# Fourth layer of a graph network: first products evicted 512 edges at a time, with one PSUM buffer more for the second products

## The chip, the core and the metric

The kernel runs on one core of a Trainium2 chip. The metric is the device time of one execution in microseconds (us), lower is better. Five engines work beside each other, each in the order of its own queue, and wait for one another through semaphores: PE (matrix products), DVE (vector work), ACT (activations, copies and casts), POOL (here only the issue of gathers and scatters) and SP (here only the issue of transfers). PE writes its products to PSUM, a small memory of its own, from which DVE and ACT read.

## What is computed

Four graph layers run over the same 12,500 nodes of 32 features and 400,000 edges sorted by their target. Each layer normalizes the nodes, forms a message for each edge, sums the messages of a node and adds the sum to it. The change lies in the fourth layer. Its edges carry 8 scalars, which a small network of two layers (8 to 256 to 256) turns into four 8x8 weight matrices for each edge:

```
h = relu(edge_scalars @ (fc_w1 / sqrt(8))) * sqrt(2)      # (E, 256): the first products
w = (h @ (fc_w2 / sqrt(256))).reshape(E, 4, 8, 8)         # (E, 256): the second products
x = node_features[edge_src]
s1, v1 = x[:, :8], x[:, 8:].reshape(E, 8, 3)
out_s = A * (einsum('eu,euw->ew', s1 * s2, w[:, 0]) + einsum('eui,ei,euw->ew', v1, v2, w[:, 1]) / sqrt(3))
out_v = B * (einsum('eu,euw,ei->ewi', s1, w[:, 2], v2) + einsum('eui,euw->ewi', v1 * s2, w[:, 3]))
node_out = segment_sum(concat(out_s, out_v), edge_dst)
```

Here s2 and v2 are the one and the three parts of the edge's 4 attributes.

## The kernel before

The fourth layer is `edges3` (from line 1252). It works in 196 windows of 2048 edges, that is 16 tiles of 128 edges, and is written out in full, without a loop at run time. For each window:

- `fetch` (SP) loads the window's edge data, `gather` (line 1274, POOL) issues one indirect transfer for each of the 16 tiles that brings the source nodes' features into `hs`. `hs` has four buffers, and the source calls `gather` two windows ahead; POOL itself goes on as soon as a buffer is free.
- `hidden(c, m, h)` forms the first products. The 256 hidden values are two halves m, the 2048 edges four quarters of B = 512. One call takes one m and two quarters: two matmuls of 512 columns (line 1285, `ps_h`) into a PSUM tile of 2 x 512 values on each partition, and one ACT instruction (line 1287) that applies relu to all 1024 and writes them to `hid`. The tile has one buffer (`ph`). Four calls make a window's `hid`.
- `product(c, g)` forms the second products of four tiles (a group g, 0 to 3): eight fp32 matmuls of 256 columns (line 1310, `ps_w`, each of them two records in the profile) into a tile of 4 x 256 values on each partition, of which there are two buffers (`pw`). Then DVE multiplies them with the gathered features in three instructions: `pa` (line 1314), `ps` (1316) and `pv` (1318). `ps` is the last to read `hs` of a group.
- `scalars` (lines 1293 to 1299, DVE) prepares `q`, `dd` and `vv` of the next window. `outputs` (1326 to 1334, DVE) sums `pa`, `pv` and `ps` of a finished window to its messages `f`.
- `thirds` splits `f` into three bf16 parts, in turns of ACT (line 472, a cast) and DVE (lines 474 and 476): cast, subtract, cast, subtract, cast.
- `places` (lines 1340 and 1341, ACT) makes the one-hot matrices `oh` from the edges' targets, with which `collect` (line 1346, PE) sums the messages into the nodes of the window; ACT copies the sums (1349), PE folds the three parts (1352), ACT copies again (1354) and sends the block to memory (`put_late`, lines 489 and 490).

The source goes through the windows with four steps s each. Step s calls `product` and `places` for this window, a part of `outputs`, `thirds`, `collect` and `add` for the last one, and `hidden` for the next one:

```python
for s in range(4):
    if now:
        product(now, s)
        places(now, 4 * s, 4 * s + 4)
    if c:
        ...
    if c + 1 < NW:
        hidden(cs[c + 1], s % 2, s // 2)
        if s == 3:
            scalars(cs[c + 1])
```

That is not the order in which the engines run it. A scheduler in the framework puts the instructions of each engine into a fixed order when the program is built, and it knows the number of buffers in each pool. For a window in the middle of the layer PE's order before is: the 16 matmuls of the collect, a `ps_h` pair, the fold, group 0, a `ps_h` pair, group 1, a `ps_h` pair, group 2, a `ps_h` pair, group 3. DVE's order is: group 3's three products of the window before, the sums (1326, 1327), group 0, the sum 1330, group 1 between 1332 and 1334, line 474, group 2, line 476, `q` and `dd`, group 3. ACT has the first cast of line 472 after the second eviction that follows the collect, and the second cast after the third.

Of the kernel before, what the change touches and what calls it, by code (L numbers as in the profile page):

```python
# [8 lines left out]
F32 = mybir.dt.float32  # L9
BF16 = mybir.dt.bfloat16  # L10
I32 = mybir.dt.int32
AF = mybir.ActivationFunctionType
ALU = mybir.AluOpType
AX = mybir.AxisListType
PSUM = bass.MemoryType.PSUM

P = 128
# [9 lines left out]
B = G * CG * P // Q4  # L27
# [29 lines left out]
class GNN:  # L57
# [1194 lines left out]
    def edges3(self):  # L1252

        nc, tc, CT = self.nc, self.tc, self.CT
        with ExitStack() as ctx:
# [1 line left out]
            gp = ctx.enter_context(tc.tile_pool(name="gather3", bufs=4))  # L1257
            wp = ctx.enter_context(tc.tile_pool(name="work3", bufs=2))
            ph = ctx.enter_context(tc.tile_pool(name="ph3", bufs=1, space=PSUM))
            pw = ctx.enter_context(tc.tile_pool(name="pw3", bufs=2, space=PSUM))  # L1260
            ps = ctx.enter_context(tc.tile_pool(name="ps3", bufs=1, space=PSUM))

            def fetch(c):
# [14 lines left out]
            def hidden(c, m, h):  # L1278

                if (m, h) == (0, 0):  # L1280
                    c["hid"] = wp.tile([P, 2, CT, Q4, 32], F32, name="hid")
                t = ph.tile([P, 2, B], F32, name="ps_h")
                for q in range(2):
                    e0 = (2 * h + q) * B
                    nc.tensor.matmul(t[:, q, :], lhsT=self.w1s[:, m * P : (m + 1) * P],
                                     rhs=c["emb"][:, e0 : e0 + B], start=True, stop=True)
                nc.scalar.activation(c["hid"][:, m, :, 2 * h : 2 * h + 2, :].rearrange("p b q s -> p q b s"),  # L1287
                                     t.rearrange("p q (b s) -> p q b s", s=32), AF.Relu)

            def scalars(c):  # L1290
                hs, sh = c["hs"], c["sh"]
# [71 lines left out]
            for s in range(4):  # L1363
                hidden(cs[0], s % 2, s // 2)
            scalars(cs[0])
            for c in range(NW + 1):
                now = cs[c] if c < NW else None
                if c + 4 < NW:
                    fetch(cs[c + 4])
                if c + 2 < NW:  # L1370
                    gather(cs[c + 2])
# [5 lines that stand above are left out]
                        last = cs[c - 1]  # L1377
                        if s == 0:
                            outputs(last)
                            self.thirds(wp, last, 0)  # L1380
                        elif s == 1:
                            self.thirds(wp, last, 1)
                            self.thirds(wp, last, 2)
                        elif s == 2:
                            self.thirds(wp, last, 3)
                            collect(last)
                        else:
                            add(last)
# [4 lines that stand above are left out]
# [156 lines left out]
```

## Time and profile before

| | |
|---|---|
| median of 3 runs | 20,938.48 us (20,915.86 to 20,953.58) |
| the profiled execution's own time | 20,931.77 us |
| its span, first to last instruction | 20,930.0 us |
| PE, DVE, ACT, POOL busy over the span | 60%, 61%, 31%, 70% |
| fourth layer, its gathers (line 1274) | 3125 gathers, 3017.6 us busy, 966 ns of one |
| second products (line 1310, PE) | 12,544 records, 3194.7 us busy |
| eviction of the first products (line 1287, ACT) | 784 x 1023 ns, 802.0 us busy |
| DVE's three products (lines 1314, 1316, 1318) | 784 x 689, 418 and 951 ns |

The profile is one execution on the chip. Its page has the busy time of each engine, the span in 40 slices with the clock that PE was granted, the DMA queues, the chain that ended last, and groups of like instructions. The trace behind it answers further: the waits (which instruction waited for which, in total, how often, the longest), the timeline of an engine in a stretch of time, and busy times by stretch. A line of the timeline gives start, duration, engine, source line, operation, the tiles by name (written <- read), the shapes, how many records were merged, and in brackets how long the engine sat idle before it and what ended that.

### The profile page before, as it was taken

How to read it: one execution, taken by the hardware profiler on the slowest of the kernel's cores; microseconds unless marked ns; L12 is line 12 of the kernel's file. 1: busy time of each engine (PE TensorE's matmuls, PEld its weight loads, DVE VectorE, ACT ScalarE, POOL GpSimd, SP SyncE). 2: the span in 40 equal slices, each digit the busy share in tenths (PEclk: the TensorE clock that was granted, in tenths of full speed). 3: DMA queues.
4: the chain of work that ended last, by engine and by line, in shares of the span. 5: the costliest groups of instructions: out<-in, count | busy, mean ns of one | idle time of the engine just before them, and what ended most of it. 6: DMA issues, size and time to landing. Idle time of an engine off the chain costs nothing.

```text
span 20930.0 us, 189759 instructions
## 1 busy us (share of the span) xinstructions
PE 12599.4 (60%) x56444; PEld 6767.2 (32%) x56444; DVE 12740.1 (61%) x25505; ACT 6408.9 (31%) x13844; POOL 14745.9 (70%) x12508
## 2 busy tenths in 40 slices
PE   2443433334766666666666666666637777777776
PEld 2333433331211111111111111111125555555554
DVE  3554444334766666666666666666746666666666
ACT  0001110002333333333333333333324444444444
POOL 5777777774788888888888888888755555555553
PEclk9999999998777777777777777777768888888888
DMA  2113332112444444444444444444411111111111
GB/s 96 46 45 111 113 91 74 23 23 72 98 89 90 88 91 90 89 89 90 90 90 90 90 90 90 90 90 90 92 39 23 23 23 23 23 23 23 23 23 30
DMA packets 1482594, 1406.96 MB, mean 67 GB/s; under 512 B 1055751, under 2 KB 1250897, under 8 KB 1426409
## 3 DMA queue, kind: packets, MB, share of 16 engines
q1 hardware_dynamic: 668550, 1143.45, 17.2%
q0 software_dynamic: 750000, 205.60, 12.0%
q10 hardware_dynamic: 62992, 45.63, 0.7%
q8 instruction: 448, 7.34, 0.1%
q14 instruction: 604, 4.94, 0.1%
HBM read 1156.82 MB, written 236.20 MB: 67 GB/s over the span
## 4 chain that ended last, share of the span: by engine, by line
DVE 27%; issue 20%; PE 15%; POOL 14%; another core or an unknown queue 13%; ACT 7%; DMA 4%; DVEq 0%; ACTq 0%; SPq 0%; POOLq 0%
DVE z L853 6%; POOL acc L1008 5%; POOL hs L809 5%; PE ps_w L1310 5%; POOL hs L535 4%; PE ps_y L850 4%; DVE pv L1318 1%; DMA hs<-feat,src_all 1%; PE ps_o L860 1%; ACT oh L1340 1%; DVE f L1327 1%; DVE pa L1314 1%; ACT X L834 1%; PE ps_sum L1346 1%
## 5 line engine op out<-in xcount | busy, mean ns | idle before, releaser
L1008 POOL DMA_INDIRECT acc<-summed,rows x3125 | 5141.5, 1645 | 999.8 <-issue 882.0
L1274 POOL DMA_INDIRECT hs<-feat,src_all x3125 | 3017.6, 966 | 2462.6 <-DVE ps L1316 1460.3
L535 POOL DMA_INDIRECT hs<-feat,src_all x3125 | 3375.3, 1080 | 1368.4 <-issue 864.4
L809 POOL DMA_INDIRECT hs<-feat,src x3125 | 3210.6, 1027 | 1190.2 <-issue 944.4
L1310 PE MATMUL ps_w<-w2b,hid 128*128 128x256 f32 x12544 | 3194.7, 411 | 68.8 <-issue 53.4
L853 DVE TENSOR_TENSOR z<-ps_y,hid 128x1024 f32<-128x1024 f32 x2352 | 2837.7, 1214 | 411.2 <-PE ps_y L850 161.2
L850 PE MATMUL ps_y<-X,w2t 64*128 64x512 f32 x4704 | 2380.0, 744 | 1132.0 <-DVE z L853 656.2
L1310 PEld LDWEIGHTS ps_w<-w2b,hid 128*128 128x128 f32 x12544 | 2577.7, 209 | 625.8 <-issue 85.8
L850 PE MATMUL ps_y<-Q,w2t 64*128 64x512 f32 x4704 | 1677.6, 838 | 1678.1 <-DVE z L853 1163.8
L460 PE MATMUL ps_win<-m,oh 128*128 128x32 f32 x6272 | 1472.7, 400 | 854.9 <-ACT m L664 211.4
L472 ACT CAST f<-f 128x512 bf16<-128x512 f32 x784 | 481.2, 614 | 4785.3 <-DVE f L878 3878.6
L860 PE MATMUL ps_o<-z,sums 128*32 128x512 f32 x9408 | 1746.1, 700 | 30.0 <-DVE r L865 21.4
L460 PEld LDWEIGHTS ps_win<-m,oh 128*128 128x128 f32 x6272 | 1396.3, 328 | 927.7 <-issue 528.3
L690 PE MATMUL ps_deg<-olo,ohi 128*125 128x100 bf16 x3136 | 462.8, 298 | 2001.6 <-DVE olo L687 1416.9
L1287 ACT ACTIVATE hid<-ps_h 128x1024 f32<-128x1024 f32 x784 | 802.0, 1023 | 2368.0 <-remote 1923.5
L1314 DVE TENSOR_TENSOR pa<-ps_w,q 128x512 f32<-128x512 f32 x784 | 540.1, 689 | 1605.5 <-remote 1407.0
L824 DVE STREAM_TRANSPOSE X<-hs 128x512 f32<-128x512 f32 x392 | 273.4, 700 | 1999.8 <-DMA hs<-feat,src 1328.8
L850 PEld LDWEIGHTS ps_y<-Q,w2t 64*128 64x128 f32 x4704 | 521.2, 256 | 2923.8 <-DVE z L853 1578.9
L850 PEld LDWEIGHTS ps_y<-X,w2t 64*128 64x128 f32 x4704 | 614.2, 210 | 2343.2 <-DVE z L853 1159.5
L663 DVE TENSOR_TENSOR m<-hs,edge_attr 128x128 f32<-128x128 f32 x784 | 228.3, 291 | 1609.6 <-issue 779.8
L664 ACT ACTIVATE m<-m 128x128 f32<-128x128 f32 x784 | 240.3, 310 | 3145.1 <-DVE m L663 1175.9
L690 PEld LDWEIGHTS <-ohi 128*125 128x125 bf16 x3136 | 445.7, 215 | 1990.8 <-DVE ohi L687 1035.7
(207 smaller groups left out, 19667.1 us busy)
## 6 DMA issues: line engine op xcount, KB each, us to landing
has<-loc_t SPq DMA_DIRECT2D x392, 1024.0 KB
srow<-in_src_t SPq DMA_DIRECT2D x392, 512.0 KB
N<-n_t SPq DMA_DIRECT2D x3136, 32.0 KB
hs<-feat,src_all POOLq DMA_INDIRECT x6250
emb<-pp SPq DMA_DIRECT2D x252, 280.0 KB
emb<-emb SPq DMA_DIRECT2D x196, 360.0 KB
emb<-pp SPq DMA_DIRECT2D x252, 224.0 KB
emb<-emb SPq DMA_DIRECT2D x196, 288.0 KB
```

The source lines that it names most:

```text
L460: nc.tensor.matmul(c["sum"], lhsT=oh[:, k, :], rhs=feat[:, k, :], start=t0 + k == 0, stop=t0 + k == self.CT - 1)
L535: self.nc.gpsimd.indirect_dma_start(out=t[:, k, :], out_offset=None, in_=self.feats[l][:], in_offset=bass.IndirectOffsetOnAxis(ap=idx[:, t ...
L690: nc.tensor.matmul(c["deg"][:NP, :J], lhsT=ohi[:, k, :], rhs=olo[:, k, :], start=t0 + k == 0, stop=t0 + k == self.CT - 1)
L809: nc.gpsimd.indirect_dma_start(out=c["hs"][:, k, :], out_offset=None, in_=self.feats[1][:], in_offset=bass.IndirectOffsetOnAxis(ap=c["src" ...
L850: nc.tensor.matmul(y[:, q, :], lhsT=self.w2t[64 * q : 64 * q + 64, h, j, :], rhs=c["Q" if j < 3 else "X"][64 * q : 64 * q + 64, h, :], sta ...
L853: nc.vector.tensor_mul(z, y, c["hid"][:, 2 * h : 2 * h + 2, :])
L860: nc.tensor.matmul(c["o", j // 3][32 * q : 32 * q + 32, :], lhsT=self.sums[:, j, :], rhs=c["z", j, q % 2][:, q // 2, :], start=j % 3 == 0, ...
L1008: nc.gpsimd.indirect_dma_start(out=self.tabs[2][k % NTAB][:], out_offset=bass.IndirectOffsetOnAxis(ap=c["rows"][:, G * g + k : G * g + k + ...
L1274: nc.gpsimd.indirect_dma_start(out=c["hs"][:, k, :], out_offset=None, in_=self.feats[3][:], in_offset=bass.IndirectOffsetOnAxis(ap=c["src" ...
L1287: nc.scalar.activation(c["hid"][:, m, :, 2 * h : 2 * h + 2, :].rearrange("p b q s -> p q b s"), t.rearrange("p q (b s) -> p q b s", s=32), ...
L1310: nc.tensor.matmul(w[:, k, :], lhsT=c["hid"][:, m, 4 * g + k].rearrange("p q s -> p (q s)"), rhs=self.w2b[:, m, :], start=m == 0, stop=m == 1)
L1314: nc.vector.tensor_mul(c["pa"][:, gs], w[:, :, 0:128].rearrange("p g (w u) -> p g w u", u=16), c["q"][:, gs, None, :].to_broadcast([P, 4, ...
```

## The change

The PSUM tile of the first products shrinks from two quarters to one, and each matmul of 512 columns has an eviction of its own, so that a window has eight evictions of 128x512 in place of four of 128x1024. The tile still has one buffer. The PSUM that this frees goes to a third buffer for the second products' tile. The sums, the products and the data are the same.

```diff
-            pw = ctx.enter_context(tc.tile_pool(name="pw3", bufs=2, space=PSUM))
+            pw = ctx.enter_context(tc.tile_pool(name="pw3", bufs=3, space=PSUM))
...
-                t = ph.tile([P, 2, B], F32, name="ps_h")
-                for q in range(2):
-                    e0 = (2 * h + q) * B
-                    nc.tensor.matmul(t[:, q, :], lhsT=self.w1s[:, m * P : (m + 1) * P],
-                                     rhs=c["emb"][:, e0 : e0 + B], start=True, stop=True)
-                nc.scalar.activation(c["hid"][:, m, :, 2 * h : 2 * h + 2, :].rearrange("p b q s -> p q b s"),
-                                     t.rearrange("p q (b s) -> p q b s", s=32), AF.Relu)
+                for q in range(2 * h, 2 * h + 2):
+                    t = ph.tile([P, B], F32, name="ps_h")
+                    nc.tensor.matmul(t, lhsT=self.w1s[:, m * P : (m + 1) * P],
+                                     rhs=c["emb"][:, q * B : (q + 1) * B], start=True, stop=True)
+                    nc.scalar.activation(c["hid"][:, m, :, q, :], t.rearrange("p (b s) -> p b s", s=32), AF.Relu)
```

The scheduler's order moves with it. In what follows h0 to h7 are the eight single `ps_h` matmuls of a window in the order in which PE has them after the change. PE then has, with the number of `ps_w` matmuls between them: the collect, the rest of group 0, h0, 2, h1, 5, h2, 3, h3, 5, h4, 2, h5, 6, h6, 1, h7, 2, and the next collect. From h1 on each of them waits for an eviction by ACT. ACT has the evictions of h4 and h5, then both casts of line 472, then the evictions of h6 and h7. DVE has `q` and `dd` after group 3, the sum 1327 (now line 1325) after group 0, and else the order above.

## The prediction

> **What bounds the kernel now.** I read the page first: the fourth layer fills the slices from about 15,400 us on, and there no engine is full. The busy times by stretch say the same: in 15,600 to 20,700 us PE is busy 3654 of 5100 us, DVE 3296, POOL 2860, ACT 2360. So this stage is bound by waits, and I read the waits of that stretch next (waiter, releaser, us in total, times, longest).
>
> ```profile
> ACT hid L1287 <- remote: 1737.7, 287, 11.5
> POOL hs L1274 <- DVE ps L1316: 1347.7, 178, 11.2
> DVE pa L1314 <- remote: 1272.6, 222, 10.2
> ...
> PEld ps_w L1310 <- DVE ps L1316: 78.8, 76, 1.0
> ...
> PEld ps_w L1310 <- DVE pv L1318: 16.9, 33, 1.0
> PE ps_w L1310 <- DVE pv L1318: 10.1, 42, 0.5
> ```
>
> PE's waits for a free ps_w buffer, which a third buffer would remove, are 79 + 17 + 10 = 106 us. The great waits are others: "remote" on DVE and ACT, 3010 us together, and POOL waiting for DVE. "Remote" means that no instruction of the profile ends where the wait ends. In the program both waiters wait for PE alone, so I put one window (512 x 4 edges, one turn of the loop) of PE, DVE, ACT and POOL side by side (start, duration, idle before).
>
> ```profile
> 18262.31 3.72 PE L1310 MATMUL ps_w<-w2b,hid 128*128 128x256 f32 x16 [0.54 <-issue]
> 18265.86 0.60 PE L1285 MATMUL ps_h<-emb,w1s 72*128 72x512 bf16 x2
> 18266.40 3.72 PE L1310 MATMUL ps_w<-w2b,hid 128*128 128x256 f32 x16
> 18278.75 1.94 PE L1346 MATMUL ps_sum<-oh,f 128*96 128x128 bf16 x16 [8.64 <-DVE f L476]
> ```
>
> ```profile
> 18266.26 0.68 DVE L474 TENSOR_TENSOR f<-f,f 128x512 f32<-128x512 f32 x1
> 18276.21 0.69 DVE L1314 TENSOR_TENSOR pa<-ps_w,q 128x512 f32<-128x512 f32 x1 [9.27 <-remote]
> ...
> 18278.02 0.68 DVE L476 TENSOR_TENSOR f<-f,f 128x512 bf16<-128x512 f32 x1
> ...
> 18279.29 0.69 DVE L1314 TENSOR_TENSOR pa<-ps_w,q 128x512 f32<-128x512 f32 x1
> ```
>
> ```profile
> 18265.51 0.62 ACT L472 CAST f<-f 128x512 bf16<-128x512 f32 x1
> 18276.26 1.02 ACT L1287 ACTIVATE hid<-ps_h 128x1024 f32<-128x1024 f32 x1 [10.13 <-remote]
> 18277.18 0.61 ACT L472 CAST f<-f 128x512 bf16<-128x512 f32 x1
> ```
>
> ```profile
> 18253.44 0.94 POOL L1274 DMA_INDIRECT hs<-feat,src_all  x1 [7.25 <-DVE ps L1316]
> ...
> 18272.38 0.95 POOL L1274 DMA_INDIRECT hs<-feat,src_all  x1 [0.30 <-issue]
> 18280.57 0.95 POOL L1274 DMA_INDIRECT hs<-feat,src_all  x1 [7.25 <-DVE ps L1316]
> ```
>
> PE finished group 2's products at 18,266.03 and the next ps_h pair at 18,266.46, yet DVE and ACT are released at 18,276.2, both at once. The word from PE (the event that tells a waiter that a product is done; its arrival is the waiter's start) is some 10 us late. What that moment goes with is POOL's stream of 16 gathers: it starts at 18,253.44, ends at 18,273.33, and 2.9 us later all held words arrive. I went through all 196 windows with the stream's start as zero. Words that PE sends up to about +7 are prompt; those of +8.5 arrive at +10 to +12, those of +10 to +11 at +14 to +20, and of those after +14 nearly all at +22.8. The four groups of a window (0 to 3) reach DVE 0, 3.3, 4.6 and 0 us late on average. The last windows, whose gathers are over, are the proof from the other side:
>
> ```profile
> 20779.35 1.06 PE L1346 MATMUL ps_sum<-oh,f 128*96 128x128 bf16 x16
> ...
> 20797.62 1.06 PE L1346 MATMUL ps_sum<-oh,f 128*96 128x128 bf16 x16
> ```
>
> There a window takes 18.3 us; with gathers it takes 27.2 (18,253.44 to 18,280.57; the median of all periods is 27.19). Why the words are late I can't see in the trace; that they are, and when, I can.
>
> So a period is a ring: DVE's last `ps` of a window frees an `hs` buffer, POOL starts its 16 gathers (20.0 us with their gaps), at +22.8 PE's words come through, and then the **tail** runs until DVE's last `ps`: 80.57 - 76.21 = 4.36 us. 22.8 + 4.4 = 27.2. Only the tail is the kernel's to change, unless PE's words no longer fall into the late stretch.
>
> **The change, part by part.** I take the orders from the built programs of both kernels, engine by engine.
>
> *Third ps_w buffer.* Removes at most the 106 us above; beside the ring it is worth nothing by itself, since PE stands idle 8.6 us waiting for L476 with two full buffers (the PE lines above). What it gives is order: PE's group 0 of the next window stands partly ahead of the collect, and DVE's q and dd (L1291, L1293 of the new file) stand behind group 3's products, not between L476 and them. That takes 79.29 - 78.62 = 0.67 us out of the tail (78.62 is L476's start and 0.60, its pitch).
>
> *ps_h in one bank, evicted by 512.* 784 evictions of 128x1024 (1023 ns) become 1568 of 128x512. That shape is not in the trace for this operation; the nearest row is L472's 128x512 cast, 614 ns, and half of 1023 is the lower bound, 512. I take 614: 4 x 2 x 0.614 = 4.9 us of ACT in a window in place of 4.1. ACT is busy 46% here, so 0.8 us is hidden, except where an eviction stands in the tail. PE's work is the same 8 matmuls.
>
> *The added waits.* With one bank, each of 8 ps_h matmuls waits for ACT's eviction of the one before; in the old kernel 4 pairs did. In the new PE order they stand 2 to 6 ps_w matmuls apart: group 0, h0, 2, h1, 5, h2, 3, h3, 5, h4, 2, h5, 6, h6, 1, h7, 2, collect. A word to ACT that is late now stops PE, with all products behind it. From the rows (0.43 us a ps_w matmul, 0.22 a ps_h one, some 0.2 until its end is known, ACT's one-hots 0.30 and L1341 0.61 from start to start), with the stream's start as zero: the collect waits for h7's eviction and ends at +0.4; fold, four products of group 0 and one of group 1 bring h0 to +3.3, h1 (after h0's eviction) to +4.4, five products h2 to +6.8. Its eviction stands behind L1341 and five one-hots, +7.5 to +8.0; three products later h3 is sent, its word at +8.7. Group 2 ends at +10.7. By the lateness above h3 reaches ACT at +10.7, its eviction ends at +11.3, h4's word goes out at +11.7 and arrives between +17 and +22.8. So h5 goes out at +18 or later and **reaches ACT at +22.8**. That step carries the forecast.
>
> *What stands behind h5 on ACT.* In the old order the first cast (L472) follows the second eviction, and ran at 18,265.51, before the held stretch; DVE's L474 ran at 18,266.26. In the new order ACT has h4, h5, cast, cast, h6, h7. DVE's L474 waits for the first cast, and group 2's products stand behind L474. So the new tail is: eviction of h5 0.52 (start to start of the next), cast 0.62, L474 0.60, group 2's three products 1.81 (76.21 to 78.02), L476 0.60, pa to the gather's start 1.28 (79.29 to 80.57) = **5.43 us, against 4.36: +1.07**. The second cast lies beside group 2's products, and ACT's register load (L489, some 0.5 us) beside h5's eviction; bare they would cost 0.6 and 0.5. If h4 too is held until +22.8, eviction 0.52, PE's h5 0.6 at the halved clock and 0.2 of hand-over come before it: 6.8 us, +2.4. h4's +11.7 lies between the stretch that arrives at 17 to 20 and the one that arrives at 22.8; I take one window in three. Mean: (2 x 1.07 + 2.4) / 3 = +1.5 us. With 188 periods of the usual length: +285 us.
>
> Bounds of that unknown: from below, no word held to +22.8 before group 3, tail then pa and ps alone (1.3 us), -3.1 a window; from above, h3 held as well, one more round of 1.35 plus group 3's matmuls at half clock, tail 9.1, +4.7 a window.
>
> Sum against the profiled execution's own time, 20,931.8 (span 20,930.0 and 1.8 around it; median of the runs 20,938.5, 0.03% above): 20,931.8 + 285 = 21,217.
>
> *Two rules weighed.* PE is idle in equal bubbles of 6 to 9 us, 27.2 us apart, and waits 106 us for PSUM. The Trainium skill, "Perfetto Trace Analysis", Identifying Performance Opportunities, says that equal bubbles can mean that buffers, PSUM among them, ran out; by it the third buffer would win much of the bubble (some 6 of 27 us). The waits contradict it. PE's granted clock is 0.84 in this stretch and 0.97 in the windows without gathers. The skill's "TensorE: Matmul & The Clock Gate", A second HAM failure mode, says that cycling through PSUM banks with small idles can throw PE to half rate; it speaks against the change; by it, taken to its end, PE's 17.95 us of work in a window at 0.87 would become 31 at 0.5 (an estimate), 3.9 us over the period, 21,660.
>
> **Rivals.**
> 1. *The words come through and PE runs ahead (faster).* If h4 arrives by about +14 and h5 by +16, group 3's products are done before +22.8, and the tail is 1.3 us: period 24.1, -3.1 x 188 = -580, 20,350; mixed with held windows, up to 20,880. For it: three buffers do put PE one group further, and early arrivals (+12 to +14) exist for words of +9.5. Against: h4 at +11.7 is 2 us too late for them, and a short period puts PE further behind the next stream. It decides from a third of the windows on: a period of 24.1 against 28.7 wins 4.6, and 0.33 x 4.6 outweighs 1.5.
> 2. *The lag grows (slower still).* Each window that ends late for PE starts the next one late; with h3 held, +2.4 to +4.7 a window: 21,400 to 21,800.
> 3. *Nothing to measure.* If in half of the windows casts get through (tail less q and dd, -0.67) and in half not (+1.07), they cancel to +0.2 a window: 20,970.
>
> **How the numbers follow.** Forecast (tail longer by 1 to 2.4): 0.55. Rival 1: 0.25. Rival 2: 0.13. Rival 3: 0.07. A measurement can tell 0.2% (42 us, 0.22 us a window) from no change. The range, 20,650 to 21,600, takes in the forecast, half of rival 1, rival 3 and the lower half of rival 2, and leaves out 0.12 below and 0.06 above. The forecast's own range is 20,980 to 21,450.
>
> **What would show it.** Right: the period between gather streams 28 to 30 us; ACT's eviction "remote" up to +22.8, then cast, L474, pa in that order; PE's waits for ACT before ps_h, 322 us now in the same stretch, grown far; waits for ps_w near none; ACT's 128x512 eviction near 0.61. Wrong: DVE's L474 and group 2 done before the stream's end, PE ahead with group 3, period under 27; or a lateness that has left the stream's clock, for instance because more words from PE change it.

## The result, and the profile after

| | old kernel | new kernel |
|---|---|---|
| median | 20,939.74 us (4 runs) | 21,494.21 us (21,490.0 to 21,501.9, 4 runs) |
| span of the profiled execution | 20,930.0 us | 21,500.2 us |
| fourth layer, group 0 of one window to group 0 of the next, mean | 27.66 us | 30.54 us |
| granted clock in the fourth layer | 0.84 | 0.83 |

The ratio is 1.0266 (95% interval 1.0249 to 1.0284): 554 us slower. A window is 2.88 us longer, and 195 such periods make 562 us: the fourth layer accounts for the whole. The forecast had the sign and the place, and half of the size (+285).

The waits of the new kernel in its fourth layer (15,700 to 21,100 us; waiter, releaser, us in total, times, longest):

```profile
DVE f L474 <- ACT f L472: 2025.0, 176, 13.1
POOL hs L1274 <- DVE ps L1314: 1860.6, 177, 12.8
...
ACT hid L1286 <- remote: 1712.8, 321, 9.4
...
PE ps_h L1284 <- ACT hid L1286: 756.9, 396, 10.1
...
PEld ps_w L1308 <- DVE pv L1316: 22.9, 41, 0.9
```

The waits for a ps_w buffer that the third buffer was to remove went from 106 to some 31 us (the 23 of the last line and 8 put down to `ps`; 39 more are put down to DVE's other instructions). Nothing was won by it. DVE's wait for late words (1273 us before, 91 now) became a wait of L474 for the cast of line 472, in all 176 windows of this stretch; POOL waits 1861 us for DVE's `ps` in place of 1348; and PE waits 757 us for ACT's evictions.

One window on ACT, the stream of gathers from 18,271.42 on (start, duration, idle before):

```profile
18285.84 0.60 ACT L1286 ACTIVATE hid<-ps_h 128x512 f32<-128x512 f32 x1 [4.48 <-remote]
...
18293.62 0.60 ACT L1286 ACTIVATE hid<-ps_h 128x512 f32<-128x512 f32 x1 [6.29 <-remote]
...
18295.46 0.58 ACT L1286 ACTIVATE hid<-ps_h 128x512 f32<-128x512 f32 x1
18297.03 0.60 ACT L1286 ACTIVATE hid<-ps_h 128x512 f32<-128x512 f32 x1 [0.99 <-PE ps_h L1284]
18297.63 0.62 ACT L472 CAST f<-f 128x512 bf16<-128x512 f32 x1
```

These are h2, h3, h4, h5 and the first cast. In this window h3 waited to +22.2, and h4 and h5 follow it in two rounds (eviction, hand-over, matmul on PE) before ACT gets to the cast. DVE and POOL after it:

```profile
18298.28 0.69 DVE L474 TENSOR_TENSOR f<-f,f 128x512 f32<-128x512 f32 x1 [10.32 <-ACT f L472]
18298.89 0.69 DVE L1312 TENSOR_TENSOR pa<-ps_w,q 128x512 f32<-128x512 f32 x1
...
18300.69 0.68 DVE L476 TENSOR_TENSOR f<-f,f 128x512 bf16<-128x512 f32 x1
18301.28 0.68 DVE L1312 TENSOR_TENSOR pa<-ps_w,q 128x512 f32<-128x512 f32 x1
```

```profile
18271.42 0.94 POOL L1274 DMA_INDIRECT hs<-feat,src_all  x1 [10.72 <-DVE ps L1314]
...
18290.70 0.94 POOL L1274 DMA_INDIRECT hs<-feat,src_all  x1 [0.30 <-issue]
18302.57 0.94 POOL L1274 DMA_INDIRECT hs<-feat,src_all  x1 [10.92 <-DVE ps L1314]
```

The order cast, L474, group 2, L476, group 3, next stream is the one forecast. The stream is about as long as it was (20.2 us here, 19.9 in the old kernel's window); what grew is the time from its end to the next one's start, from 7.2 to 10.9 us.

### The profile page after: what moved, and what is told of

Read it like the earlier page. It is cut to its first block, busy times and chain, and to the rows that moved or that the text cites. A ratio compares the mean times of both kernels' runs of the same rounds, so it can differ in the third digit from the quotient of the medians.

```text
span 21500.2 us, 190349 instructions
## 1 busy us (share of the span) xinstructions
PE 12926.1 (60%) x56444; PEld 6863.8 (32%) x56444; DVE 12738.6 (59%) x25505; ACT 6548.3 (30%) x14628; POOL 14743.3 (69%) x12508
## 4 chain that ended last, share of the span: by engine, by line
PE 21%; DVE 17%; issue 13%; ACT 9%; POOL 9%; another core or an unknown queue 8%; DMA 2%; DVEq 0%; ACTq 0%; POOLq 0%; SPq 0%
PE ps_w L1308 11%; DVE z L853 6%; POOL hs L809 5%; POOL acc L1008 4%; PE ps_y L850 4%; ACT hid L1286 3%; PE ps_h L1284 2%; ACT oh L1338 2%; PE ps_o L860 1%; ACT X L834 1%; ACT oh L1339 1%; DVE cnt L990 1%; DVE X L824 1%; DVE summed L1004 1%
## 5 line engine op out<-in xcount | busy, mean ns | idle before, releaser
L1308 PE MATMUL ps_w<-w2b,hid 128*128 128x256 f32 x12544 | 3696.7, 438 | 49.5 <-ACT hid L1286 49.0
L1308 PEld LDWEIGHTS ps_w<-w2b,hid 128*128 128x128 f32 x12544 | 2744.8, 223 | 2720.1 <-issue 1996.9
L1284 PE MATMUL ps_h<-emb,w1s 72*128 72x512 bf16 x1568 | 686.5, 438 | 1985.7 <-issue 968.2
L1286 ACT ACTIVATE hid<-ps_h 128x512 f32<-128x512 f32 x1568 | 934.2, 596 | 2839.4 <-remote 1920.5
L474 DVE TENSOR_TENSOR f<-f,f 128x512 f32<-128x512 f32 x392 | 269.2, 687 | 2173.4 <-ACT f L472 2173.2
```

The lines of the kernel that those rows point to most:

```text
L1284: nc.tensor.matmul(t, lhsT=self.w1s[:, m * P : (m + 1) * P], rhs=c["emb"][:, q * B : (q + 1) * B], start=True, stop=True)
L1286: nc.scalar.activation(c["hid"][:, m, :, q, :], t.rearrange("p (b s) -> p b s", s=32), AF.Relu)
L1308: nc.tensor.matmul(w[:, k, :], lhsT=c["hid"][:, m, 4 * g + k].rearrange("p q s -> p (q s)"), rhs=self.w2b[:, m, :], start=m == 0, stop=m == 1)
```

## The experiments

Theory: the loss comes through PE's late words. A late word holds one eviction on ACT until the stream has ended, and each round of eviction, hand-over and matmul that the one bank puts behind that eviction lengthens the period. Rivals: the one bank costs by itself; the third ps_w buffer is to blame; the casts alone make the tail. By the tail I mean, as in the prediction, the time from the late word to the next stream of gathers.

The chips differ. On four of the five that ran the experiments PE's words are prompt: the old kernel takes 18,920 to 18,937 us there, and in the traces of the experiments there "remote" is not in the fourth layer's list of waits. The two kernels of the result, and the last two runs below, ran where the old kernel takes 20,908 to 20,940. So each run is compared with the old kernel on its own chip.

### Where words are prompt: the new kernel, the one bank, two single banks

`a1_after_again` is the new kernel unchanged. `e1_one_bank_two_pw` and `e2_two_single_banks` change its pools:

```diff
 e1
-            pw = ctx.enter_context(tc.tile_pool(name="pw3", bufs=3, space=PSUM))
+            pw = ctx.enter_context(tc.tile_pool(name="pw3", bufs=2, space=PSUM))
 e2, besides
-            ph = ctx.enter_context(tc.tile_pool(name="ph3", bufs=1, space=PSUM))
+            ph = ctx.enter_context(tc.tile_pool(name="ph3", bufs=2, space=PSUM))
```

> The new kernel unchanged, once more, beside the old one. Theory (all of the loss comes through PE's late words): where the old kernel takes about 20,940 us again, the new one is 2.7% slower again; where PE's words come at once (the old kernel near 18,930, the gathers end to end, no idle time of ScalarE put down to 'remote'), both kernels are held by POOL's 16 gathers of 1.25 us, 20.5 us a window, and the new one is within 0.3% of the old. Rival (the one bank has a price of its own): slower by 1% or more there too.

> The new kernel with two buffers for ps_w again; the one-bank ps_h with its 128x512 evictions stays. Theory (a wait for each eviction costs: every ps_h matmul waits for an eviction whose start hangs on a late word from PE, so that h4 and h5 go out a round late): the third ps_w buffer has hardly any part in the loss; period between gather streams 30 us or more, 21,400 to 21,700 us. Rival (the third buffer's part in PE's order and banks is to blame): back near 20,940, period near 27.

> ps_h of one bank each, but two buffers of it, and two of ps_w: the same eight 128x512 evictions, but a ps_h matmul waits for the eviction of the last but one. Theory (the wait for the eviction just before is what costs): most of the loss goes, period 26.5 to 28.5 us, 20,800 to 21,200. Rival (smaller evictions and twice as many words from PE to ScalarE cost by themselves): stays at 21,350 to 21,600.

Measured: a1 18,855.21 us, 0.9961 of the old kernel (0.9947 to 0.9975); e1 18,938.03, 1.0004 (0.9995 to 1.0014); e2 18,924.5, 0.9998 (0.9989 to 1.0008). None of the numbers expected of e1 and e2 holds, since the lateness that both theories took for granted was not there. What they show is something else. **With prompt words the same change is 70 us faster, not 554 slower** (0.39%, a little past the 0.3% expected of a1). The one bank alone (e1) costs nothing that shows there, so the gain goes with the third buffer and the order that the scheduler makes with it (a1 and e1 ran on two chips, 13 and 6, whose old kernels agree within 5 us; the last section has what differs between the two). From a1, POOL's largest wait in 15,000 to 18,600 us, and from its page the line of the gathers (count, us busy, mean ns, idle before):

```profile
POOL hs L1274 <- issue: 822.9, 2700, 0.3
```

```profile
L1274 POOL DMA_INDIRECT hs<-feat,src_all x3125 | 2975.7, 952 | 1060.3 <-issue 897.6
```

POOL bounds the layer here: nearly all of its idle time before gathers is the 0.3 us between one and the next, and a window takes 20.1 us, 16 gathers of 1.25. The eviction of 128x512 takes 592 ns (596 in the new kernel's first profile; the prediction took 614).

### No gathers

`e3_before_no_gathers` and `e4_after_no_gathers`, in the old and in the new kernel; the fourth layer then sums other rows:

```diff
-                for k in self.rows_for(c["hs"], CT, c, 0):
-                    nc.gpsimd.indirect_dma_start(
-                        out=c["hs"][:, k, :], out_offset=None, in_=self.feats[3][:],
-                        in_offset=bass.IndirectOffsetOnAxis(ap=c["src"][:, k : k + 1], axis=0))
+                nc.sync.dma_start(c["hs"], self.feats[3][: P * CT].rearrange("(p t) d -> p t d", t=CT))
```

> The old kernel, with the 16 indirect gathers of a fourth-layer window replaced by one plain load of the feature rows in their order (the sums are then those of other rows). Theory (PE's words are late only while a gather stream runs): ScalarE's idle time on PE's words nearly gone, window 18 to 19 us, about 20,940 less 8.5 x 190, so 19,300 (19,100 to 19,600). Rival (the words are late because PE, ScalarE and VectorE hold each other up in this order): period stays above 25 us, over 20,500.

> The new kernel with the same replacement. Theory (the new waits cost only because the words are late): within 0.5 us a window of the old kernel with plain loads, so within 100 us of it. Rival (the one bank costs by itself, 8 rounds of matmul, hand-over and eviction of about 1 us each in PE's path): 1 to 3 us a window more than the old kernel with plain loads, 200 to 560 us.

Measured on a chip with prompt words: 18,399.22 and 18,399.39 us; a window takes 17.81 and 17.80 us. The number for e3 missed, because there was no lateness to take away (18,930 to 18,399 is POOL's bound, 20.5 to 17.8 us a window). That the two kernels agree within 1 us is what e4's theory expected, and it counts against the rival's 200 to 560 us. It doesn't show that the eight evictions and their waits are free: DVE is busy 3167 and 3165 of the 3200 us from 15,000 to 18,200, so it bounds both kernels, and what ACT and PE lose beside it can't show.

### The lateness made by hand

To test the tail where words are prompt, an eviction of my choice was made to wait for the stream: ACT reads one element of the last tile that POOL is gathering.

```diff
+            def hold(c):
+                if 0 < c["no"] < NW - 2:
+                    late = wp.tile([P, 1], F32, name="late")
+                    nc.scalar.copy(late, cs[c["no"] + 2]["hs"][:, CT - 1, 0:1])
...
+                    if (m, q) == (0, 2):
+                        hold(c)
                     nc.scalar.activation(c["hid"][:, m, :, q, :], t.rearrange("p (b s) -> p b s", s=32), AF.Relu)
...
-                if c + 2 < NW:
-                    gather(cs[c + 2])
+                if c + 3 < NW:
+                    gather(cs[c + 3])
```

This is `m4_after_held_h4`, with h4 held. `m0_before_held` holds the old kernel's third pair, the one that was late to +22.9; `m5_after_held_h5` was meant to hold h5; `m4w2_held_h4_two_pw` is m4 with two ps_w buffers.

> A lateness made by hand: the old kernel, in which ScalarE, ahead of the third eviction of a window (the one that was held to the stream's end), copies one element of the last tile that POOL gathers during that window (three windows ahead), so that this eviction, and what stands behind it on ScalarE, waits until the stream has landed, on any chip. Theory (the period is the stream, 20.0, some 2 to 3 us to landing, and the tail from the third eviction to VectorE's last ps, 4.4 us): period 26 to 28 us, 20,000 to 20,400 us where the unheld kernel takes 18,925. Rival (the late words cost by something else): period under 23.5.

> The new kernel with the same copy ahead of the sixth of its eight evictions, the one that the prediction took to be the first held to the stream's end. Theory: tail of the prediction's sum, 5.4 in place of 4.4 us: 1 to 1.5 us a window and 200 to 300 us more than the old kernel held. Rival (it is not the tail that makes the new kernel slower): within 60 us of the old kernel held, or faster.

> The new kernel with the same copy ahead of the fifth eviction, the one that was held to the stream's end in the measured kernel. Theory (one more round of eviction, hand-over, matmul in the tail): 2.4 to 3.4 us a window and 450 to 650 us more than the old kernel held, the size of the measured loss. Rival (the tail is set by the casts, not by the rounds): same as with the sixth held, within 60 us.

> As the last, with two ps_w buffers. Theory (all of the loss is the one bank's): within 100 us of the kernel with three, since in the tail the products stand behind the evictions, not behind ps_w. Rival (the third buffer, which lets PE run further ahead, has a part in the loss, or saves some of it): over 200 us away, in either direction.

Measured: m0 20,265.78 us (1.0710 of the old kernel, 1.0679 to 1.0742), period 27.39, as expected, where the old kernel with words late by themselves had 27.66. But its tail is not the old kernel's. ACT in m0:

```profile
17027.15 0.19 ACT L1281 COPY late<-hs 128x1 f32<-128x1 f32 x1 [9.20 <-DMA hs<-feat,src_all]
17027.25 0.61 ACT L472 CAST f<-f 128x512 bf16<-128x512 f32 x1
17027.77 1.02 ACT L1294 ACTIVATE hid<-ps_h 128x1024 f32<-128x1024 f32 x1
```

The scheduler put the copy ahead of the first cast too. In the old kernel that cast had run before the held stretch, at 18,265.51 in the prediction's window. (Counted from the collect it stands behind the third eviction there, not behind the second.) The copy starts at +21.15 (median), 1.7 us ahead of the +22.8 of the late words, and the next stream starts 6.2 us after it, where the old kernel has a tail of 4.4: two differences that nearly cancel. So the casts are held in m0 as they are in the new kernel, and what a run has above m0 is not the price of the casts.

m4 20,586.87 (1.0880, 1.0849 to 1.0912), 321 above m0; its theory expected 450 to 650. m5 20,600.8 (1.0888), no different, but it told nothing: the scheduler had put the copy ahead of h4, and the order was m4's. m4w2 20,930.14, 343 above m4. It missed the 100 us of its theory: with the lateness made by hand, the third buffer, with the order that comes with it, saves time.

The next run fixed the place, with h4's result as a second operand of the copy (`m5b_after_held_h5`), and two more followed, with the copy's result, times nought, as the held eviction's bias: h3 held (`m3_after_held_h3`), and h4 held in the kernel with two single banks (`m2h4_two_single_banks_held`).

```diff
 m5b, ahead of h5
+                    nc.scalar.activation(late, cs[c["no"] + 2]["hs"][:, CT - 1, 0:1], AF.Identity, bias=c["hid"][:, 0, 0, 2, 0:1])
 m3 (ahead of h3) and m2h4 (ahead of h4)
+                    nc.scalar.activation(late, cs[c["no"] + 2]["hs"][:, CT - 1, 0:1], AF.Identity, scale=0.0)
```

> The copy ahead of the sixth eviction of the new kernel again, now with the fifth eviction's result as a second operand, so that it can't stand ahead of the fifth (in the run with the sixth held, the scheduler had put it there: its order was that of the kernel with the fifth held). Theory (each round of eviction, hand-over and matmul behind the held word is in the tail): about 1.3 us a window less than with the fifth held, 20,587 less 250, so 20,300 to 20,400, within 150 us of the old kernel held. Rival (the casts and group 2 behind them set the tail, and the rounds lie beside them): within 60 us of 20,590.

> The new kernel with the fourth eviction held until the stream has landed (the copy's result, times nought, is that eviction's bias, so that its place is fixed). The three kernels held so far differ by one round: sixth held 20,272, fifth held 20,587. Theory (every round of eviction, hand-over and matmul behind the held word adds 315 us): 20,800 to 21,000, some 630 above the old kernel held (20,266); the measured loss of 554 then lies between the fifth and the fourth held. Rival (the casts and products cover any further round): within 100 us of 20,587.

> Two single banks for ps_h and two ps_w buffers, the fifth eviction held in the same way; beside it stands the kernel with one single bank and two ps_w buffers, held at the same place, 20,930. Theory (it is the wait of each ps_h matmul for the eviction just before it that puts a round into the tail; with two banks the sixth matmul is done when the hold ends): 300 us or more below that, 20,250 to 20,630. Rival (twice as many evictions cost, whatever the banks): within 100 us of 20,930.

| held | time, us | ratio to the old kernel beside it | above m0 | period, us |
|---|---|---|---|---|
| old kernel, third pair (m0) | 20,265.78 | 1.0710 (1.0679 to 1.0742) | | 27.39 |
| new, h5 (m5b) | 20,272.09 | 1.0713 (1.0692 to 1.0734) | 6 | 27.38 |
| new, h4 (m4) | 20,586.87 | 1.0880 (1.0849 to 1.0912) | 321 | 29.05 |
| new, h3 (m3) | 20,955.84 | 1.1068 (1.1036 to 1.1100) | 690 | 30.85 |
| h4, two ps_w buffers (m4w2) | 20,930.14 | 1.1062 (1.1029 to 1.1094) | 664 | 30.81 |
| h4, two single banks, two ps_w (m2h4) | 20,902.74 | 1.1040 (1.1008 to 1.1072) | 637 | 30.59 |

m3's time lies in its theory's range; m5b's lies 28 us under it, and within 150 us of m0 as expected. m3 and m2h4 ran on chip 8, the others on chip 3; the old kernel takes 14 to 17 us more on chip 8. ACT behind the copy, first in m5b, then in m4, then in m3:

```profile
17034.75 0.29 ACT L1281 ACTIVATE late<-hs,hid 128x1 f32<-128x1 f32 x1 [8.60 <-DMA hs<-feat,src_all]
17034.95 0.58 ACT L1293 ACTIVATE hid<-ps_h 128x512 f32<-128x512 f32 x1
17035.43 0.61 ACT L472 CAST f<-f 128x512 bf16<-128x512 f32 x1
```

```profile
17037.05 0.19 ACT L1281 COPY late<-hs 128x1 f32<-128x1 f32 x1 [9.36 <-DMA hs<-feat,src_all]
17037.15 0.59 ACT L1293 ACTIVATE hid<-ps_h 128x512 f32<-128x512 f32 x1
17038.41 0.60 ACT L1293 ACTIVATE hid<-ps_h 128x512 f32<-128x512 f32 x1 [0.67 <-PE ps_h L1289]
17039.01 0.62 ACT L472 CAST f<-f 128x512 bf16<-128x512 f32 x1
```

```profile
17048.28 0.20 ACT L1281 ACTIVATE late<-hs 128x1 f32<-128x1 f32 x1 [11.22 <-DMA hs<-feat,src_all]
...
17049.88 0.60 ACT L1294 ACTIVATE hid<-ps_h 128x512 f32<-128x512 f32 x1 [0.67 <-PE ps_h L1290]
17052.01 0.60 ACT L1294 ACTIVATE hid<-ps_h 128x512 f32<-128x512 f32 x1 [1.54 <-PE ps_h L1290]
17052.51 0.61 ACT L472 CAST f<-f 128x512 bf16<-128x512 f32 x1
```

From the copy to the cast it is 0.68, 1.96 and 4.23 us. Each eviction held earlier puts one more round there, and in m3 two ps_w matmuls stand between h4 and h5 besides. The period grows by 1.67 us from m5b to m4 and by 1.80 from m4 to m3. What PE has left to do behind h5 is a smaller part of it; its six ps_w matmuls (12 records) in m5b, then in m4:

```profile
17026.44 2.75 PE L1315 MATMUL ps_w<-w2b,hid 128*128 128x256 f32 x12
```

```profile
17038.17 5.33 PE L1315 MATMUL ps_w<-w2b,hid 128*128 128x256 f32 x12
```

With h5 held they are done while ACT waits (its copy starts at 17,034.75); with h4 held they come after it, and at half the pace (0.44 against 0.23 us a record; PE had stood idle for 8.9 us). DVE's group 3 waits for them 0.25 us a window on average in m4, and never in m5b. So the theory of the rounds holds: the casts and group 2 stand behind the hold in all three, and each round more makes the time longer all the same. The casts alone don't make the loss. That they are free isn't shown: m5b is as fast as m0 because m0 holds the casts too. The traces of the result give both shares; they stand below.

m2h4 went against its theory (27 us from m4w2, 300 expected). It can't settle the point, because with these pools the scheduler puts h4 to h7 together and all eight products of group 3 behind them: the wait for the eviction was gone and more of PE's work stood behind the held one. What two single banks would do in the order of the new kernel stays open.

### The gathered rows as one tile

`e5_before_ring_tile` and `e6_after_ring_tile`, the old and the new kernel:

```diff
-            gp = ctx.enter_context(tc.tile_pool(name="gather3", bufs=4))
+            gp = ctx.enter_context(tc.tile_pool(name="gather3", bufs=1))
+            ring = gp.tile([P, 4 * CT, D], F32, name="hs")
...
-                c["hs"] = gp.tile([P, CT, D], F32, name="hs")
+                c["hs"] = ring[:, c["no"] % 4 * CT : (c["no"] % 4 + 1) * CT, :]
```

> The old kernel, with the four buffers of gathered rows as one tile, so that a gather waits for VectorE's last reader of its own four tiles of the window and not for the whole buffer: the stream of 16 gathers breaks into parts of four. Theory (PE's words are held while POOL issues gathers without a pause, and let through when it stops): with stops between the parts the words come within a part, some 5 us, period 21 to 24 us, 600 to 1,200 us less than the old kernel where that takes 20,940. Rival (they are held by the number of gathers, not by the stream's lack of a pause): within 200 us of the old kernel. Where words are not late at all: within 50 us of 18,930, since POOL then bounds both.

> The new kernel with the four buffers of gathered rows as one tile, so that a gather waits for the readers of its own rows only. Where PE's words come at once: POOL's 16 gathers bound both, 18,800 to 18,870, that is 0.996 of the old kernel as the new one has. Where they come late (the old kernel at 20,940): theory (held while POOL issues without a pause) 800 us or more below the old kernel; rival (held by the number of gathers) within 200 us of the new one, 21,490.

With prompt words: e5 18,923.77 us, 1.0001 (0.9991 to 1.0012); e6 18,854.47, 0.9963 (0.9949 to 0.9977). The tile alone changes nothing there, as expected of a layer that POOL bounds.

### Where the words are late by themselves, once more

The last pair repeats e1 and e6, and found a chip with late words: the old kernel takes 20,907.75 us there.

> One bank and two ps_w buffers once more. Where PE's words are late by themselves (old kernel at 20,940): theory (the third buffer gives back part of what the one bank costs) 21,600 to 21,900, above the new kernel's 21,494; rival (the third buffer is what costs) 20,940 to 21,300. Where they are prompt: 18,930, as before.

> The new kernel with the gathered rows as one ring tile once more. Where PE's words are late by themselves: theory (held while POOL issues without a pause) under 20,700; rival (held by the number of gathers) 21,300 to 21,600. Where they are prompt: 18,855, as before.

Measured: e1_b 21,502.59 us, 1.0285 (1.0255 to 1.0315), period 30.62. Both numbers expected of it missed: with two ps_w buffers the kernel is as slow as with three (1.0266, 1.0249 to 1.0284). **So the one bank makes the loss also without the third buffer**; what the buffer saved with the lateness made by hand (343 us), it does not save here. Holding one eviction is not the whole of what late words do. And equal times are not equal tails: the scheduler's order is another one with two buffers. In e1_b L474 starts at +20.4 (median) and not at +25.6, and DVE's group 3 then waits 2.3 us a window for PE, against 0.15 in the new kernel. From the waits of e1_b (15,700 to 21,100 us):

```profile
DVE pa L1312 <- PE ps_w L1308: 577.4, 275, 3.5
```

So it isn't shown that the third buffer changes nothing, only that it isn't needed for the loss.

e6_b 20,605.92 us, 0.9856 (0.9828 to 0.9885), as its theory expected: 302 us under the old kernel beside it, 888 under the new one's 21,494. This version beats both kernels where words are late, and is level with the new one where they are prompt. Three of its waits (15,700 to 20,300 us):

```profile
POOL hs L1275 <- DVE ps L1315: 1055.8, 364, 9.1
ACT s L1348 <- remote: 866.7, 131, 11.5
...
ACT hid L1287 <- remote: 199.7, 71, 4.7
```

POOL stops 364 times for DVE in place of 177, for 2.9 us on average in place of 10.5. ACT's evictions wait 200 us for late words in place of 1713. Words are still late, now those of the collect. A part of the gather also starts sooner, as soon as its own group of the window is read; the run doesn't separate the two gains. The period is 25.9 us, still above the 20.1 at which POOL bounds this kernel with prompt words.

## Why the prediction was half right

**The ring, the sign and the tail's sum: right.** Stream, lateness by the stream's clock, the order cast, L474, group 2, L476, group 3: as forecast; the period, 30.5 in the median, lies just above the 28 to 30 named as a sign. From h5's eviction to the next stream it is 5.54 us in the median of the new kernel's 176 windows from 15,700 to 21,100 us (forecast 5.43), from h4's 7.10 (forecast 6.8); the old kernel's tail is 4.36. So casts and order make some 1.2 us of the longer tail, and h4's round 1.6. h2, sent at +8.7 in the median, arrives at +12.2; h3, sent at +13.2, at +20.7; h4, sent at +22.0, at +23.0.

**The step that failed: "the collect waits for h7's eviction and ends at +0.4".** It ends at +2.0: h7's eviction itself ends at +0.4, and a ps_w matmul and the collect's own 16 come after it. From there all is shifted: h0 at +5.2 (forecast +3.3), h1 at +6.3 (+4.4), h2 at +8.7 (+6.8). By the forecast h2 was just early enough to be prompt; at +8.7 it falls into the late words and comes 3.6 us late, and PE, which now waits for each eviction, sends h3 at +13.2, not +8.7. So in the typical window h3 was held to +20.7, and h4's word, forecast at +11.7, went out at +22.0. It reached ACT at +22 or later in all 176 windows, and h5 went out only then; the forecast had h5 there, and h4 in one window of three.

**The term that was mis-sized: the mean of the two tails.** (2 x 1.07 + 2.4) / 3 = +1.5 took h4 as held in one window of three, and it is held in all. What a held h5 and a held h4 cost was right within 0.3 us. On average h4's eviction starts at +23.49 and 7.12 us lie behind it, 30.61 in all; in the old kernel group 2's word comes at +23.01 and 4.60 lie behind it, 27.61. Of these 3.0 us (by the starts of the streams in this stretch; 2.88 by group 0 over the layer) 2.5 are tail, and 0.5 is h4 itself, which a late h3 pushes past the +22.8 at which it would have come. The forecast had "h3 held too" as its second rival, 21,400 to 21,800 us, at 0.13. The time fell into that range, but h3 came at +22 or later in 53 of the 176 windows only; in the others the earlier lateness of h3 was enough to hold h4.

**Rival 1 (PE runs ahead): did not come.** Its condition, words that come through, is met only on the four chips where no word is late. There the change is faster, by 70 us and not by 580, because POOL's 16 gathers of 1.25 us bound the window; and 60 of the 83 us between a1 and e1 go with shorter gathers (last section), not with PE running ahead.

**The eviction: right.** 596 ns, taken as 614. Outside the tail its price doesn't show, since DVE (e3 and e4) or POOL (a1) bounds the window there.

**The two rules.** The Trainium skill, "Perfetto Trace Analysis", Identifying Performance Opportunities, says that equal bubbles can mean too few buffers. Here they did not: the waits for PSUM went from 106 to 31 us, and no time was won with late words. The granted clock in the layer is 0.83 in the new kernel with late words, 0.85 with h4 held by hand and 0.96 with prompt words, for the same matmuls. With the gathers left out, where PE hardly waits, it is 1.00. So in these runs it goes with the idle time, and not with the buffers. The Trainium skill, "TensorE: Matmul & The Clock Gate", A second HAM failure mode, tells of a kernel whose clock swings between half and full rate because cycling through PSUM banks leaves PE small idles; a1, with its eight single-bank evictions, is at 0.96 on average.

**Open:** why PE's words are late, and why on some chips only. The first three layers do the same work in 14,796 us on chips with prompt words (the first gather of the fourth layer starts then in m0) and in 15,396 on the other, so it is not this layer's alone. No run told whether it stays with a chip. Open too is what two single banks would do where words are late, and which of its two gains makes e6_b faster.

## What to carry to other kernels

A producer that may get ahead by one buffer only turns each late hand-over into a full round, and the rounds behind the last late one are added to the period; count those, for the position in which the producer really stands and not for the one before it shifts, and count in how many windows each case holds. A wait that is added by hand holds all that the scheduler puts behind it: read the order of the engine before comparing it with another run (m0 held the casts too, m5 held h4). Where a wait is put down to nothing in the program, time the kernel on more than one chip before tuning for it: here the sign of the change depended on it. A buffer that is given back in the parts in which it is read lets a producer start sooner and breaks its long streams; in e5 and e6 it cost nothing where it won nothing.

## What was not expected of the hardware

- The same kernel takes 18,920 to 18,937 us on four chips and 20,908 to 20,940 on others, with the same gathers of 0.95 to 0.97 us. In the fourth layer the difference stands in the waits as "remote": some 3010 us in the old kernel where words are late, none in the traces where they are prompt.
- Where POOL bounds the layer, its gathers take 971 ns in e1 and 952 in a1; 3125 x 19 ns is 60 of the 83 us between the two. In e1's fourth layer 343 of the 370 gathers that overlap DVE's L474 in time took over 1.03 us; in a1, where L474 falls elsewhere against the gathers, 19 of 212. This was seen and not tested.
